# Splitting delta into bfloat16 pieces by the upper halves of its words, with a new plan for the stages between the scans

## The chip, the cores and the metric

The kernel runs on one core of a Trainium2 chip. The metric is device time in microseconds for one execution of the whole program. Before the change the median of 3 runs was 10320.08 us (10318.13 to 10324.31).

## The reference

The input `x` is 8 images of 96 channels and 64 x 64 pixels. Two layers follow. The first is a vision state-space block with four scan directions; the second is linear attention in six heads and a feed-forward net with 8-bit and 16-bit rounding. Cut to what matters here:

```python
# layer 0, per image: L = 4096 pixels, 192 channels, 4 directions k, 16 states n
xz = layernorm(gn(x)) @ in_proj_w.T + in_proj_b      # split into xi and z
xi = silu(depthwise_conv3x3(xi))
xs = four orders of xi                               # rows, columns, and both reversed
dts, Bs, Cs = split(einsum('bkdl,kcd->bkcl', xs, x_proj_w))
delta = softplus(dt_proj(dts) + dt_proj_b)
h[t] = exp(delta[t] * A) * h[t-1] + (delta[t] * u[t]) * B[t]
y[t] = sum over n of C[t] * h[t] + D * u[t]
x = x + (layernorm(sum of the four y) * silu(z)) @ out_proj_w.T + out_proj_b
# layer 1, per image
t = t + linear_attention(layernorm(t))
t = t + ffn(layernorm(t))
```

`delta` is needed twice by the scan: multiplied with the input (`delta * u`), and multiplied with the decay rates `A` under an exponential. The kernel does the second product on TensorE in bfloat16, and keeps its precision by writing each float32 `delta` as a sum of three bfloat16 pieces.

## The kernel before

The images are worked in four pairs. The program is a row of stages: a planned stage for pair 0, the scan of pair 0, a planned stage that finishes pair 0 and prepares pair 1, the scan of pair 1, and so on; a fifth planned stage finishes pair 3. So there are five planned stages and four scans. `scan` (from line 696) is written out by hand, an instruction list of 32 chunks x 4 directions; it reads `delta`'s pieces (`dl`), `delta * u` (`du`) and the states (`bs`, `cs`) from HBM and writes `ys`.

A planned stage is recorded as a list of operations first. `Plan.add` takes for each the engine, a cost in microseconds written in the call, what it reads and writes, which ring of buffers it needs, and a rank (a due time). `Plan.run` then emits the operations: among those that could start within 0.1 us of the earliest on each engine it takes the one of lowest rank, it advances each engine's clock by the written cost, and adds 1.3 us when ScalarE has to change its table of functions. So the costs and ranks decide the order of the instructions on each engine, and nothing else. The chip's engines and the one DMA queue (SP) then take their instructions strictly in that order.

A middle stage holds these parts for the pair that is finished and the pair that is begun:

- `project` (line 419): group norm, layer norm and input projection, 16 chunks of 512 pixels. Ranks rise from 0 to `FRONT`.
- `convolve` (line 513): the depthwise convolution, two thirds on VectorE (lines 537 and 540, 36 instructions of about 1.3 to 2.4 us), one third on TensorE. Ranks from `FRONT` to `CONV`.
- `prepare` (line 587): 32 sets (4 directions x 8 chunks) of 3 tiles of 128 x 512, so 96 tiles. Ranks from `PREP` to 1. A set begins with two matmul groups (lines 637 and 657) that give the states and `delta`'s argument. Each tile then takes: a softplus on ScalarE into `d`; the product `d * u` on VectorE (line 670), which is stored as `du`; and the split of `d` into three pieces in `dp`, stored as `dl`. For the second and fourth direction GpSimd first transposes `u` (line 624).
- `back` (line 935): 16 units, from the sum of the four `ys` (line 982) over the transposition by TensorE (line 996), a layer norm, the gate, the output projection (line 1015) and the attention's sums. Ranks from 0 to `BACK`.
- `tail` (line 1081): 16 units that begin when all of `back` is done; each ends in a store to `out` from GpSimd's last addition (line 1132). Ranks from `TAIL` to `TAIL_END`.

The first stage has no `back` and `tail`, the last has nothing else. The split, as it stands before:

```python
act(..., P[dp][:, :, 0], w(d), AF.Copy, 0.62, ...)                       # ScalarE rounds d
dve(..., tensor_tensor(w(rest), w(d), P[dp][:, :, 0], ALU.subtract))     # line 681, VectorE
act(..., P[dp][:, :, 1], w(rest), AF.Copy, 0.63, ...)                    # ScalarE rounds rest
P.add("POOL", ..., tensor_tensor(P[dp][:, :, 2], w(rest), P[dp][:, :, 1], ALU.subtract))  # line 686
```

Rings limit how many tiles are on their way: three buffers each of `d`, `du` and `dp`, two of `rest`. All stores and loads are issued by SP (line 315), in one queue. The profile names the buffers of the prepare part and of the projection `A`, those of the tail `yd` and `yk`, because they share memory; line 296 is the helper that records every activation.

Of the kernel before, what the change touches and what calls it, by code (L numbers as in the profile page):

```python
# [12 lines left out]
BF16 = mybir.dt.bfloat16  # L13
F8 = mybir.dt.float8e5
AF = mybir.ActivationFunctionType
ALU = mybir.AluOpType
# [3 lines left out]
DIM = 96  # L20
# [17 lines left out]
HQ = TC // 4  # L38
FRONT = 0.13
CONV = 0.27  # L40
PREP = 0.15
BACK = 0.63
TAIL = 0.85
TAIL_END = 1.33
NE = 24
X0 = F - 3 * SEG
WC = 256
# [123 lines left out]
def vss_attn_ffn(ctx: ExitStack, tc: tile.TileContext, a: dict):  # L171
    nc = tc.nc
# [232 lines left out]
    def norm(P, n, src_, read, dst, written, new, hold, rank, **kw):  # L405

        mm(P, 0.9, lambda: nc.tensor.matmul(P["ncp" + n][:DIM], c96, src_(), start=True, stop=True),  # L407
           (read, "w_c96"), ("ncp" + n,), (("ncp" + n, hold),), rank)
        act(P, lambda: P["nsq" + n], lambda: P["ncp" + n][:DIM], AF.Square, 0.6, ("ncp" + n,),
            ("nsq" + n,), (("nsq" + n, "small"),), rank)  # L410
        mm(P, 0.9, lambda: nc.tensor.matmul(  # L411
            P["nvp" + n][:DIM], j96, P["nsq" + n], start=True, stop=True),
           ("nsq" + n, "w_j96"), ("nvp" + n,), (("nvp" + n, "q"),), rank)
# [99 lines left out]
    def convolve(P, xi, ybuf, p1, beside):  # L513
# [10 lines left out]
        for h in range(2):  # L524
# [20 lines left out]
            def taps(h, ns):  # L545
# [11 lines left out]
            P.claims.add(len(P.ops))  # L557
            mm(P, 9.0, lambda h=h, ns=ns, taps=taps: taps(h, ns),
               ("edge1", *[f"pad1#{c}" for c in range(NCH) if h or c <= NCH // 2],
# [27 lines left out]
    def prepare(P, tmp, xi, us, dl, du, bs, cs_, beside):  # L587
# [25 lines left out]
        for o in range(2):  # L613
            for c in range(NCH):
# [14 lines left out]
                for k in (o, o + 2):  # L629
# [3 lines left out]
                    def states(pt, k, u):  # L633
# [8 lines left out]
                    P.unit = f"set.{k}.{c}"  # L642
                    mm(P, 1.9, lambda pt=pt, k=k, u=u, states=states: states(pt, k, u),
                       (*un[0], *un[1], *un[2], "xw"), (pt,), ((pt, "q"),), rank)
# [10 lines left out]
                    def steps_(pqs, k, S):  # L655
# [5 lines left out]

                    mm(P, 1.2, lambda pqs=pqs, k=k, S=S, steps_=steps_: steps_(pqs, k, S),
                       (S, *[f"dtw{at}" for at, *_ in places]), pqs, [(q, "q") for q in pqs], rank)
                    P.unit = None
                    for T in range(3):
                        m = f"{n}.{T}"
                        pq, d, q, dp, rest = "pq" + m, "d" + m, "du" + m, "dp" + m, "rest" + m
                        act(P, lambda d=d: P[d], lambda pq=pq: P[pq], AF.Softplus, 0.675, (pq, "w_dtb"), (d,),
                            ((d, "d"),), rank, "softplus", bias=dtb[:, k, half(T) : half(T) + 1])
                        dve(P, 0.88, lambda q=q, d=d, f=u[T]: nc.vector.tensor_tensor(  # L670
                            P[q], P[d], f(), ALU.mult), (d, *un[T]), (q,), ((q, "du"),), rank)
                        j = slice(c * F // TC, (c + 1) * F // TC)
                        spread(P, 0.26, lambda o, n, k=k, j=j: duv[k, j, o : o + n].rearrange("j p t -> p j t"),
                               T, lambda q=q: P[q].rearrange("p (j t) -> p j t", t=TC), (q,), (), rank)

                        def w(name):
                            return P[name].rearrange("p (j t) -> p j t", t=WC)

                        act(P, lambda dp=dp: P[dp][:, :, 0], lambda d=d, w=w: w(d), AF.Copy, 0.62, (d,),
                            (dp + "#0",), ((dp, "dp"),), rank)  # L680
                        dve(P, 0.88, lambda rest=rest, d=d, dp=dp, w=w: nc.vector.tensor_tensor(  # L681
                            w(rest), w(d), P[dp][:, :, 0], ALU.subtract), (d, dp + "#0"), (rest,),
                            ((rest, "rest"),), rank)
                        act(P, lambda dp=dp: P[dp][:, :, 1], lambda rest=rest, w=w: w(rest), AF.Copy, 0.63,
                            (rest,), (dp + "#1",), (), rank)
                        P.add("POOL", 1.24, lambda rest=rest, dp=dp, w=w: nc.gpsimd.tensor_tensor(  # L686
                            P[dp][:, :, 2], w(rest), P[dp][:, :, 1], ALU.subtract), (rest, dp + "#1"),
                            (dp + "#2",), (), rank)
                        spread(P, 0.39, lambda o, n, k=k, c=c: dlv[
                                   k, c * F // WC : (c + 1) * F // WC, :, o : o + n  # L690
                               ].rearrange("j a p t -> p (j a) t"),
                               T, lambda dp=dp: P[dp].rearrange("p j a t -> p (j a) t"),
                               (dp + "#0", dp + "#1", dp + "#2"), (), rank)
# [241 lines left out]
    def back(P, pair, ys, us, zs, t1, tn, tmp, psm, kept=None):  # L935
# [21 lines left out]
        for i in range(2 * NCH):  # L957
# [55 lines left out]
            def both(dst, src_, w):  # L1013
                for g in range(2):
                    nc.tensor.matmul(P[dst][:DIM], w(g), P[src_][:, g], start=(g == 0), stop=(g == 1))  # L1015

            mm(P, 1.8, lambda mean=mean, yt=yt, both=both: both(mean, yt, lambda g: j192),
               (f"{yt}#0", f"{yt}#1"), (mean,), ((mean, "q"),), rank)
            for g in range(2):
# [3 lines left out]
                    (f"{yt}#{g}",), (f"{g_}#{g}",), ((g_, "g"),), rank)  # L1023
            mm(P, 1.8, lambda yv=yv, g_=g_, both=both: both(yv, g_, lambda g: j192),
               (f"{g_}#0", f"{g_}#1"), (yv,), ((yv, "q"),), rank)
            root(P, n, yv, yrs, "small", rank)
            for g in range(2):
# [5 lines left out]
                    (z3,), (f"{g_}#{g}",), (), rank)  # L1033
            mm(P, 1.8, lambda po=po, g_=g_, both=both: both(po, g_, lambda g: woT[:, g]),
               (f"{g_}#0", f"{g_}#1"), (po,), ((po, "q"),), rank)
# [7 lines left out]
            for h in range(2):  # L1043
# [15 lines left out]

                mm(P, 0.7, lambda pk=pk, to=to, h=h, keys=keys: keys(pk, to, h), (to,), (pk,), ((pk, "q"),), rank)  # L1060
                act(P, lambda kv=kv: P[kv].rearrange("p j s e -> p (j s e)"), lambda pk=pk: P[pk][:, : 4 * DIM],
# [19 lines left out]
    def tail(P, pair, t1, tn, spare, kept):  # L1081
# [10 lines left out]
        for i in range(2 * NCH):  # L1092
# [9 lines left out]
            else:  # L1102
                tf, xa = f"tnsb.{i}", f"tab.{i}"
            P.unit = f"turn.{n}"
            mm(P, 0.9, lambda pa=pa, b=b, tf=tf: nc.tensor.matmul(
                P[pa][:DIM], hm[b], P[tf], start=True, stop=True), (tf, f"hm{b}"), (pa,), ((pa, "q"),), rank)
# [4 lines left out]
            for m in range(3):  # L1111
                p1, h16 = f"pf{m}" + n, f"h16{m}" + n
                mm(P, 0.45, lambda p1=p1, m=m, tq=tq: nc.tensor.matmul(  # L1113
                    P[p1], w1q[:, bass.ts(m, 128)], P[tq], start=True, stop=True), (tq,), (p1,), ((p1, "q"),), rank)
# [7 lines left out]
            def second(p2, hq):  # L1122
                for m in range(3):
                    nc.tensor.matmul(P[p2][:DIM], w2q[:, m], P[hq][:, m], start=(m == 0), stop=(m == 2))

            mm(P, 1.35, lambda p2=p2, hq=hq, second=second: second(p2, hq),
               [f"{hq}#{m}" for m in range(3)], (p2,), ((p2, "q"),), rank)
# [186 lines left out]
```

## Time and profile before

| what | value |
|---|---|
| median of 3 runs | 10320.08 us |
| the profiled execution's own time | 10309.3 us |
| its span, first to last instruction | 10307.5 us |
| planned stages (five) | 0 to 553, 2329 to 3106, 4880 to 5641, 7415 to 8186, 9962 to 10307 us |
| scans (four) | the rest, 1774 to 1776 us each |
| busy share of the span: TensorE, VectorE, ScalarE, GpSimd | 71%, 88%, 68%, 78% |
| L681, VectorE remainder, x384 | 324.2 us, mean 851 ns, median 685 ns |
| L686, GpSimd remainder, x384 | 489.2 us, mean 1280 ns, median 1155 ns |
| L670, product with u, two forms of x192 | means 851 and 1080 ns |
| table loads on ScalarE | 155 x 1283 ns |
| granted TensorE clock, mean | 0.873 |

How to read the views: a group's line gives the source line, the engine, the operation and its tiles, then the busy time and the mean of one instruction. A line of the waits says which engine and line waited for which, the time in total, how often, and the longest. A row by stretch gives, for a piece of the span, the busy time of TensorE (PE), its weight loads (PEld), VectorE (DVE), ScalarE (ACT) and GpSimd (POOL), each with its count of instructions, then the granted TensorE clock, the mean busy share of the DMA engines and the rate they moved. A row of the timeline gives the start, the duration, the engine, the line and operation, and in brackets how long the engine had stood idle and what it had waited for.

### The profile page before, as it was taken

To read this page: it belongs to the slowest core of one execution; us is meant where nothing else is said; L and a number is where in the kernel's file an instruction comes from. 1 tells how busy PE (TensorE), PEld (TensorE's weight loads), DVE (VectorE), ACT (ScalarE), POOL (GpSimd) and SP (SyncE) were. 2 spreads that over 40 slices of the span, in tenths; PEclk is the share of its full clock that TensorE was granted. 3 is DMA by queue.
4 is the path that set the end of the run, shared out by engine and by line. 5 is a ranking of instruction groups with operands and counts; after the bars stand their busy time and mean duration, and the time that the engine had idled before them with its cause. 6 is when DMAs were issued, how large, how long until landed. Compare 5 with 4: busy or idle time off the path is not lost. (4 is left out here: it accounts for less than half of the span.)

```text
span 10307.5 us, 383249 instructions
## 1 busy us (share of the span) xinstructions
PE 7289.4 (71%) x166080; PEld 5185.1 (50%) x166080; DVE 9045.2 (88%) x6688; ACT 7000.9 (68%) x12268; POOL 8011.6 (78%) x2800
## 2 busy tenths in 40 slices
PE   6766666768866666676886666767688567666678
PEld 2155555654315555555432555656543255555554
DVE  6589999997579999999767999999866799999985
ACT  5667777776566777776666777777666677777754
POOL 2499999991259999999125999999713699999971
PEclk7579999898868999989986989898898798999999
DMA  4878887876778888887787788888767788888885
GB/s 127 226 210 214 213 216 212 218 203 146 209 205 210 215 213 217 213 217 189 171 210 203 213 217 212 217 212 217 194 165 206 200 214 214 214 215 216 214 193 104
DMA packets 1593918, 2085.12 MB, mean 202 GB/s; under 512 B 409891, under 2 KB 1050404, under 8 KB 1588644
## 3 DMA queue, kind: packets, MB, share of 16 engines
q1 hardware_dynamic: 1592228, 2060.59, 76.6%
q8 instruction: 1304, 21.36, 1.0%
q14 instruction: 386, 3.16, 0.1%
HBM read 1601.99 MB, written 458.04 MB: 200 GB/s over the span
## 5 line engine op out<-in xcount | busy, mean ns | idle before, releaser
L853 DVE TENSOR_TENSOR_SCAN h<-da,dbu 128x774 f32<-128x774 f32 x4096 | 7026.6, 1759 | 168.1 <-POOL dbu L817 33.1
L817 POOL TENSOR_TENSOR dbu<-dut,bc 128x1536 f32<-128x1536 f32 x2048 | 7081.8, 3572 | 71.8 <-DMA dm<-dl 35.9
L842 ACT ACTIVATE da<-da 128x768 f32<-128x768 f32 x4092 | 3260.7, 797 | 1983.9 <-PE da L835 1969.5
L835 PE MATMUL da<-dm,aw 128*128 128x128 bf16 x24576 | 2281.5, 235 | 2347.3 <-DVE h L853 2081.8
L835 PEld LDWEIGHTS <-aw 128*128 128x128 bf16 x24576 | 1792.2, 104 | 2595.2 <-issue 2308.8
L871 PE MATMUL yp<-h,cw 128*32 128x48 f32 x131072 | 2899.2, 238 | 83.7 <-issue 70.3
L871 PEld LDWEIGHTS yp<-h,cw 128*32 128x32 f32 x131072 | 2409.0, 154 | 528.6 <-issue 207.5
L771 ACT ACTIVATE cw<-bc,blk 128x512 f32<-128x512 f32 x2048 | 1473.1, 721 | 73.0 <-DMA bc<-cs 54.7
L686 POOL TENSOR_TENSOR A<-A 128x512 bf16<-128x512 f32 x384 | 489.2, 1280 | 954.5 <-ACT A L296 912.0
L296 ACT ACTIVATE A<-A 128x512 bf16<-128x512 f32 (+1 forms) x777 | 466.4, 620 | 274.0 <-DVE A L681 228.4
L982 POOL TENSOR_TENSOR yd<-yk 128x768 f32<-128x768 f32 x64 | 120.8, 1888 | 655.3 <-PE q L996 306.4
L879 ACT ACTIVATE yev<-yp 128x384 f32<-128x384 f32 x1024 | 504.7, 493 | 74.6 <-PE yp L871 74.3
L681 DVE TENSOR_TENSOR A<-A 128x512 f32<-128x512 f32 x384 | 324.2, 851 | 174.7 <-ACT A L296 135.7
L814 ACT COPY dbu<-h 128x12 f32<-128x12 f32 x1984 | 409.3, 206 | 0.0
L657 PE MATMUL q<-A 6*64 6x512 f32 x1536 | 331.6, 779 | 74.3 <-ACT A L296 70.4
L624 POOL COPY A<-A 128x512 f32<-128x512 f32 x96 | 142.5, 1504 | 307.8 <-ACT A L296 277.3
L540 DVE SCALAR_TENSOR_TENSOR A<-A,c_convw,A 128x2048 f32<-128x2048 f32 x128 | 299.1, 2355 | 0.6
L996 PEld LDWEIGHTS q<-ident,yd 128*96 128x96 f32 x2048 | 238.6, 165 | 84.1 <-issue 53.1
L670 DVE TENSOR_TENSOR A<-A 128x512 f32<-128x512 f32 x192 | 203.8, 1080 | 77.3 <-ACT A L296 70.8
L996 PE MATMUL q<-ident,yd 128*96 128x128 f32 x2048 | 255.1, 276 | 17.3 <-DVE yd L982 9.5
L637 PE MATMUL q<-A 128*64 128x512 f32 x512 | 209.5, 935 | 77.3 <-ACT A L296 56.6
L296 ACT ACTIVATE small<-hold 96x512 f32<-96x512 f32 x192 | 112.7, 590 | 218.5 <-PE hold L407 218.3
(125 smaller groups left out, 5446.5 us busy)
## 6 DMA issues: line engine op xcount, KB each, us to landing
dut<-du SPq DMA_DIRECT2D x2048, 384.0 KB
dm<-dl SPq DMA_DIRECT2D x1024, 288.0 KB
dl<-A SPq DMA_DIRECT2D x256, 384.0 KB
dm<-dl SPq DMA_DIRECT2D x1024, 96.0 KB
ys<-yev SPq DMA_DIRECT2D x1024, 96.0 KB
du<-A SPq DMA_DIRECT2D x256, 256.0 KB
bc<-cs SPq DMA_DIRECT2D x512, 128.0 KB
bc<-bs SPq DMA_DIRECT2D x512, 128.0 KB
```

What stands on the lines that cost most here:

```text
L296: "ACT", cost, lambda: nc.scalar.activation(dst(), src_(), func, **kw),
L657: nc.tensor.matmul(P[pqs[T]][o : o + 64], dtw[at : at + RK, k, o : o + 64], P[S][at : at + RK], start=True, stop=True,)
L686: P.add("POOL", 1.24, lambda rest=rest, dp=dp, w=w: nc.gpsimd.tensor_tensor(P[dp][:, :, 2], w(rest), P[dp][:, :, 1], ALU.subtract), (rest, ...
L771: nc.scalar.activation(cw[i % 2][:, :, :, m, :].rearrange("p z j t -> p (z j) t"), bc[i][:, 1].rearrange("p z (j t) -> p (z j) t", j=NB), ...
L814: nc.scalar.copy(start, segs(hs[s - 1][:, :, r])[:, :, :, 1 if back else TC])
L817: nc.gpsimd.tensor_tensor(segs(t)[:, :, :, 1:], dut[g].unsqueeze(1) .to_broadcast([128, 2, NI, TC]), bc[s // NB][:, 0, :, bass.ts(c % NB, ...
L835: nc.tensor.matmul(e[:, i], aw[k, r][:, i, z, :], dm[s // 2][:, NI * r + i, bass.ts(c % 2, TC)], start=True, stop=True,)
L842: nc.scalar.activation(e, e, AF.Exp)
L853: nc.vector.tensor_tensor_scan(hs[s][:, w, r][:, d], da[p % 3][:, o : o + W6][:, d], dbu[4 * s + r][:, w][:, d], 0.0, ALU.mult, ALU.add,)
L871: nc.tensor.matmul(y[32 * q : 32 * q + 32, 2 * NE * i : 2 * NE * i + 2 * NE] .rearrange("p (j r i) -> p i j r", j=2, r=NR), w[:, z, :, t], ...
L879: nc.scalar.activation(yev[s][:, :, o : o + 8, :].rearrange("p j i e -> p i j e"), y[:, 0 : 16 * NE].rearrange("p (i j e) -> p i j e", j=2 ...
L996: nc.tensor.matmul(o, P[yd][:, k, j, DIM * g : DIM * g + DIM], ident, start=(k + j == 0), stop=(k + j == 4),)
```

## The change

The change has two parts.

First, the split. A bfloat16 number is the upper half of a float32 word. The new `high(name)` looks at a float32 tile as 2-byte values and takes every second one, so it is the word with its lower half cut off. The first remainder is then `d - high(d)` and the second `rest - high(rest)`; both are VectorE instructions, and neither reads `dp`. ScalarE's two copies of the halves into `dp` stay, and no later remainder reads them. GpSimd's remainder is gone. Pieces are now cut off instead of rounded.

Second, the plan. Six ranks get other values. Costs written for TensorE's groups go up in most places (1.9 to 2.85 and 1.2 to 2.1 in a set, 9.0 to 10.5 for the convolution's taps) and down in two of the tail's. The cost of VectorE's product goes from 0.88 to 0.66, and that of ScalarE's copies from 0.62 and 0.63 to 0.56. These numbers change only the order in which the planned stages' instructions stand.

```diff
-FRONT = 0.13
-CONV = 0.27
-PREP = 0.15
-BACK = 0.63
-TAIL = 0.85
-TAIL_END = 1.33
+FRONT = 0.05
+CONV = 0.35
+PREP = 0.08
+BACK = 0.7
+TAIL = 0.66
+TAIL_END = 1.29
...
-                    mm(P, 1.9, lambda pt=pt, k=k, u=u, states=states: states(pt, k, u),
+                    mm(P, 2.85, lambda pt=pt, k=k, u=u, states=states: states(pt, k, u),
...
-                    mm(P, 1.2, lambda pqs=pqs, k=k, S=S, steps_=steps_: steps_(pqs, k, S),
+                    mm(P, 2.1, lambda pqs=pqs, k=k, S=S, steps_=steps_: steps_(pqs, k, S),
...
-                        dve(P, 0.88, lambda q=q, d=d, f=u[T]: nc.vector.tensor_tensor(
+                        dve(P, 0.66, lambda q=q, d=d, f=u[T]: nc.vector.tensor_tensor(
...
-                        act(P, lambda dp=dp: P[dp][:, :, 0], lambda d=d, w=w: w(d), AF.Copy, 0.62, (d,),
+                        def high(name):
+                            return P[name].bitcast(BF16).rearrange("p (j t o) -> p j t o", t=WC, o=2)[:, :, :, 1]
+
+                        dve(P, 0.66, lambda rest=rest, d=d, w=w, high=high: nc.vector.tensor_tensor(
+                            w(rest), w(d), high(d), ALU.subtract), (d,), (rest,), ((rest, "rest"),), rank)
+                        act(P, lambda dp=dp: P[dp][:, :, 0], lambda d=d, high=high: high(d), AF.Copy, 0.56, (d,),
                             (dp + "#0",), ((dp, "dp"),), rank)
-                        dve(P, 0.88, lambda rest=rest, d=d, dp=dp, w=w: nc.vector.tensor_tensor(
-                            w(rest), w(d), P[dp][:, :, 0], ALU.subtract), (d, dp + "#0"), (rest,),
-                            ((rest, "rest"),), rank)
-                        act(P, lambda dp=dp: P[dp][:, :, 1], lambda rest=rest, w=w: w(rest), AF.Copy, 0.63,
+                        dve(P, 0.66, lambda rest=rest, dp=dp, w=w, high=high: nc.vector.tensor_tensor(
+                            P[dp][:, :, 2], w(rest), high(rest), ALU.subtract), (rest,),
+                            (dp + "#2",), ((dp, "dp"),), rank)
+                        act(P, lambda dp=dp: P[dp][:, :, 1], lambda rest=rest, high=high: high(rest), AF.Copy, 0.56,
                             (rest,), (dp + "#1",), (), rank)
-                        P.add("POOL", 1.24, lambda rest=rest, dp=dp, w=w: nc.gpsimd.tensor_tensor(
-                            P[dp][:, :, 2], w(rest), P[dp][:, :, 1], ALU.subtract), (rest, dp + "#1"),
-                            (dp + "#2",), (), rank)
```

The other lines of the diff change costs alone: the norm's matmuls 0.9 to 1.03, the taps 9.0 to 10.5, the back half's pairs 1.8 to 2.0, its keys 0.7 to 0.86, the tail's first matmul 0.9 to 1.2, its second 0.45 to 0.4 and its third 1.35 to 1.15. The lines below the split stand two lines further down in the new file: the tail's addition on GpSimd is line 1134 there, and the two new remainders are lines 682 and 686.

More of the change, by code (lines that the diff above doesn't have):

```diff
@@ L405, in norm @@
     def norm(P, n, src_, read, dst, written, new, hold, rank, **kw):
-        mm(P, 0.9, lambda: nc.tensor.matmul(P["ncp" + n][:DIM], c96, src_(), start=True, stop=True),
+        mm(P, 1.03, lambda: nc.tensor.matmul(P["ncp" + n][:DIM], c96, src_(), start=True, stop=True),
            (read, "w_c96"), ("ncp" + n,), (("ncp" + n, hold),), rank)
@@ L410, in norm @@
             ("nsq" + n,), (("nsq" + n, "small"),), rank)
-        mm(P, 0.9, lambda: nc.tensor.matmul(
+        mm(P, 1.03, lambda: nc.tensor.matmul(
             P["nvp" + n][:DIM], j96, P["nsq" + n], start=True, stop=True),
@@ L557, in convolve @@
             P.claims.add(len(P.ops))
-            mm(P, 9.0, lambda h=h, ns=ns, taps=taps: taps(h, ns),
+            mm(P, 10.5, lambda h=h, ns=ns, taps=taps: taps(h, ns),
                ("edge1", *[f"pad1#{c}" for c in range(NCH) if h or c <= NCH // 2],
@@ L1015, in both @@
                     nc.tensor.matmul(P[dst][:DIM], w(g), P[src_][:, g], start=(g == 0), stop=(g == 1))
-            mm(P, 1.8, lambda mean=mean, yt=yt, both=both: both(mean, yt, lambda g: j192),
+            mm(P, 2.0, lambda mean=mean, yt=yt, both=both: both(mean, yt, lambda g: j192),
                (f"{yt}#0", f"{yt}#1"), (mean,), ((mean, "q"),), rank)
@@ L1023, in back @@
                     (f"{yt}#{g}",), (f"{g_}#{g}",), ((g_, "g"),), rank)
-            mm(P, 1.8, lambda yv=yv, g_=g_, both=both: both(yv, g_, lambda g: j192),
+            mm(P, 2.0, lambda yv=yv, g_=g_, both=both: both(yv, g_, lambda g: j192),
                (f"{g_}#0", f"{g_}#1"), (yv,), ((yv, "q"),), rank)
@@ L1033, in back @@
                     (z3,), (f"{g_}#{g}",), (), rank)
-            mm(P, 1.8, lambda po=po, g_=g_, both=both: both(po, g_, lambda g: woT[:, g]),
+            mm(P, 2.0, lambda po=po, g_=g_, both=both: both(po, g_, lambda g: woT[:, g]),
                (f"{g_}#0", f"{g_}#1"), (po,), ((po, "q"),), rank)
@@ L1058, in outer @@
                         )
-                mm(P, 0.7, lambda pk=pk, to=to, h=h, keys=keys: keys(pk, to, h), (to,), (pk,), ((pk, "q"),), rank)
+                mm(P, 0.86, lambda pk=pk, to=to, h=h, keys=keys: keys(pk, to, h), (to,), (pk,), ((pk, "q"),), rank)
                 act(P, lambda kv=kv: P[kv].rearrange("p j s e -> p (j s e)"), lambda pk=pk: P[pk][:, : 4 * DIM],
@@ L1104, in tail @@
             P.unit = f"turn.{n}"
-            mm(P, 0.9, lambda pa=pa, b=b, tf=tf: nc.tensor.matmul(
+            mm(P, 1.2, lambda pa=pa, b=b, tf=tf: nc.tensor.matmul(
                 P[pa][:DIM], hm[b], P[tf], start=True, stop=True), (tf, f"hm{b}"), (pa,), ((pa, "q"),), rank)
@@ L1112, in tail @@
                 p1, h16 = f"pf{m}" + n, f"h16{m}" + n
-                mm(P, 0.45, lambda p1=p1, m=m, tq=tq: nc.tensor.matmul(
+                mm(P, 0.4, lambda p1=p1, m=m, tq=tq: nc.tensor.matmul(
                     P[p1], w1q[:, bass.ts(m, 128)], P[tq], start=True, stop=True), (tq,), (p1,), ((p1, "q"),), rank)
@@ L1124, in second @@
                     nc.tensor.matmul(P[p2][:DIM], w2q[:, m], P[hq][:, m], start=(m == 0), stop=(m == 2))
-            mm(P, 1.35, lambda p2=p2, hq=hq, second=second: second(p2, hq),
+            mm(P, 1.15, lambda p2=p2, hq=hq, second=second: second(p2, hq),
                [f"{hq}#{m}" for m in range(3)], (p2,), ((p2, "q"),), rank)
```

## The prediction

> **What bounds the kernel now.** I read the page's busy shares first, then its 40 slices, then the busy time by stretch, then the waits inside the stretches that the change touches, and last the order of the instructions.
>
> ```profile
> DVE  6589999997579999999767999999866799999985
> POOL 2499999991259999999125999999713699999971
> DMA  4878887876778888887787788888767788888885
> ```
>
> The slices show two kinds of stage. Where POOL reads 9 the selective scan runs: VectorE is busy 99 us of each 100 and GpSimd 100. Four such scans take 4 x 1775 us, and the change touches none of their instructions. Between them lie five planned stages, 0 to 553, 2329 to 3106, 4880 to 5641, 7415 to 8186 and 9962 to 10307 us: together 3207 us. There no engine is full, so I ask which wait ends last. The next view has the busy time by stretch (PE, PEld, DVE, ACT, POOL, then clock, DMA share, GB/s): first the prepare part of the first stage, then the second stage in four parts.
>
> ```profile
> 225.00:525.00 300.00, 218.02 (x600) 44.43 (x596) 173.44 (x193) 181.26 (x314) 136.13 (x114) 0.59 0.87 225
> 2329.00:2575.00 246.00, 200.53 (x1423) 105.70 (x1416) 173.63 (x188) 156.77 (x237) 25.74 (x27) 0.90 0.65 151
> 2575.00:2760.00 185.00, 159.71 (x699) 80.30 (x697) 91.34 (x131) 93.42 (x155) 36.78 (x27) 0.88 0.79 209
> 2760.00:3075.00 315.00, 234.94 (x720) 63.55 (x720) 226.77 (x321) 234.88 (x398) 153.99 (x114) 0.71 0.77 208
> 3075.00:3106.00 31.00, 3.06 (x24) 2.52 (x25) 6.13 (x4) 8.41 (x13) 11.76 (x6) 0.50 0.59 150
> ```
>
> I call the four parts of the second stage A (projection and convolution), C (most units of the layer's back half, with the first prepared tiles), D (the rest of the tiles, with the tail units) and E (the scan's start). In D every engine is at 49 to 75% and the DMA below the 225 GB/s of the first stage. What stops them is each other:
>
> ```profile
> POOL A L686 <- ACT A L296: 133.6, 48, 7.2
> ACT A L296 <- DVE A L681: 34.4, 35, 3.3
> DVE A L681 <- ACT A L296: 20.2, 17, 2.6
> ```
>
> ```profile
> SPq L315 <- DVE A L670: 30.5, 25, 3.6
> SPq L315 <- POOL A L686: 29.5, 26, 4.7
> SPq L315 <- ACT A L296: 12.8, 14, 1.7
> ```
>
> The split of delta goes ScalarE, VectorE, ScalarE, GpSimd, store: ScalarE's copy waits for VectorE's remainder and the reverse, and the store queue, served in order, waits for products (L670) and last remainders (L686). SP's waits in D sum to about 103 us. GpSimd also slows VectorE:
>
> ```profile
> 359.55 1.16 POOL L686 TENSOR_TENSOR A<-A 128x512 bf16<-128x512 f32 x1 [2.38 <-ACT A L296]
> 360.08 1.17 DVE L670 TENSOR_TENSOR A<-A,A 128x512 f32<-128x512 f32 x1 [1.33 <-ACT A L296]
> 361.18 0.68 DVE L681 TENSOR_TENSOR A<-A 128x512 f32<-128x512 f32 x1
> ```
>
> A subtraction alone takes 0.68 us, a product begun under L686 1.17. The group means hide this: L681 has median 0.685 and mean 0.851, L670 means 0.851 and 1.080 in its two forms.
>
> **The change, part by part.** A planned stage has 32 sets of 3 tiles, 96 tiles.
>
> *Removed:* 96 x 1.274 us (489.2/384) = 122 us of GpSimd work a stage. It costs GpSimd nothing to lose, but it takes one crossing off the way to each store.
>
> *Added:* 96 remainders on VectorE. Nearest row: L681 without a neighbour, 0.685, so 66 us a stage. Relief in return: L681 96 x 0.166 = 16; L670's first form 48 x 0.167 = 8; of the second form's excess of 0.396 I keep half, since L624's copies remain on GpSimd, 48 x 0.198 = 9.5. Net +33 us a stage.
>
> *Strided halves:* both subtractions and both copies now read 2-byte values 4 bytes apart. No row shows that. The Trainium skill (SBUF — State Buffer, the cachelines note) says that a stride is free while two accesses fall on one 16-byte line; here four do, so I take nothing added: copies 0.62, subtractions 0.685. The upper bound doubles the time per element: VectorE (0.976 for 768 elements, 0.684 for 512) gives 1.14 ns, so +0.58 us an instruction; ScalarE (0.797 for 768, 0.62 for 512) 0.69 ns, so +0.35. Below nothing, a copy of 16-bit data could save some 0.03 us (the f16 evictions took 0.59), 6 us a stage.
>
> *Table loads:* the order shows 54 instead of 47 on ScalarE in each middle stage, 14 and 14 in the first. The row is 1.283 us, and the next activation in D follows at once (a load at 2989.69, work at 2990.99). The skill (ScalarE: Activation LUTs, What ACT_TABLE_LOAD costs) adds a drain of 1.38 us to every switch. By the row, 7 x 1.28 = 9 us; by the rule, 19. I take the row, half of it hidden since ScalarE was busy 75% of D: +5.
>
> *First stage.* The tiles leave at 3.1 us each (300/96). A set stores 1152 KB of pieces, 768 of products and 128 of states: 0.70 MB a tile, 67 MB at 225 GB/s. SP waits for producers only 50 us of 270, in pieces under 1 us mostly. So the DMA bounds this stretch, and the shorter chain only lifts it to what its best 25 us show, 235 GB/s: 300 x (1 - 225/235) = -13. Bounds: 0, and -35 at the 255 GB/s of D's best slices. The prepare part starts no earlier: VectorE still has nearly all 36 convolution steps ahead of its first product.
>
> *Middle stages.* By the order, the old stage has about 21 tiles multiplied when the 16th back unit ends and 75 after it; the new one 36 and 60. It also has one back unit less ahead of the convolution's end. And after the last tile four `out` stores of tail units follow, with the scan's loads behind them on SP; before, only stores of tiles followed the last `out`.
> - A loses one back unit, some 8.4 us of VectorE (0.98 + 2 x 0.74 + 2 x 0.68 + 2 x 0.84 + 2 x 0.75 + 0.74 + 0.69), which was busy there: -9.
> - C gains this unit, 12.8 us of TensorE (205 us for 16 in the last stage), and 15 tiles. TensorE takes 1.94 + 1.67 us a set when warm, so 5 sets 18 us, at C's 86% 21: +34.
> - D loses 15 tiles at 3.1: -46. The rest, 269 us, goes from 208 to the first stage's 225 GB/s as SP's waits shrink: -20. VectorE then has 227 - 27 + 41 - 21 = 220 us in 249, 88%; the convolution stretch shows it at 91%, so it just fits.
> - The end: today the scan's memsets stand between the last tiles:
>
> ```profile
> 3065.14 6.92 POOL L714 MEMSET cw<- 128x8192 f32 x1 [0.48 <-DMA out_dram<-yk]
> 3070.33 6.88 DVE L713 MEMSET cw<- 128x8192 f32 x1 [1.70 <-issue]
> 3072.02 7.86 POOL L686 TENSOR_TENSOR A<-A 128x512 bf16<-128x512 f32 x2
> 3077.14 0.62 DVE L681 TENSOR_TENSOR A<-A 128x512 f32<-128x512 f32 x1
> ```
>
> The last tile's pieces wait for two memsets; in the new order the memsets follow all tiles: -12. But four tail units stay uncovered. The last stage does 16 in 90 us, so 4 x 5.6 = +22.
> Sum: -9 + 34 - 66 - 12 + 22 + 5 = -26, times 3 = -78.
>
> *Last stage:* only its plan changes; TensorE is busy 203 of 218 us in its first part, whatever the order: 0. Scans: 0, though the first loads wait on what ended the stage before.
>
> Total -91 on the profiled execution's own 10309.3 us (span 10307.5): 10218. The median of the runs shown, 10320.08, lies 11 us above that execution, so I forecast 10230.
>
> **Rivals.**
> - *More is freed (0.15).* If D runs at its best slices, 255 GB/s, and C hides the added tiles under TensorE's idle 14%, a middle stage loses 50 and the first 25: 10320 - 175 = 10145, say 10160. For it: SP's 103 us of waits. Against: VectorE at 88%.
> - *The transfers are the limit anyway (0.13).* D stays at 208 GB/s: 3 x 20 and the first stage's 13 vanish, leaving -18 to -30: 10295. For it: DMA shares of 0.77 to 0.87 are near what the stages ever hold.
> - *The uncovered tails eat it (0.12).* A tail unit is a chain of some 30 us; if none of the last four has begun when the last tile leaves, 45 us a stage lie bare instead of 22, and the gain is 22: 10298 to 10325, no change.
> - *The strided halves cost a second turn (0.15), the slower case.* VectorE's pair and ScalarE's pair, in D and the first stage. D's 60 tiles add 60 x 2 x 0.58 = 70 us to VectorE, which then needs 290 us, at 91% 319 instead of 249; C adds about 4. So 74 - 26 = +48 a middle stage, and some +20 in the first: 10320 + 164 = 10485. It decides from about 0.2 us more per instruction, that is when the two remainders average 0.9 us or above. Half of it gives 10390.
> - That the change doesn't do what it says: GpSimd's remainders are gone from its list and VectorE has 96 more a stage, so this is only open for the durations.
>
> **How the numbers follow.** The likeliest case, 10190 to 10280, has 0.45. A measurement of this kernel can tell about 0.2% (21 us) from no change, so the bounds are 10299 and 10341. Faster: 0.45 + 0.15 + most of the 0.13 = 0.72; the rest of that and the tails case give the same, 0.13; slower 0.15. From 10160 to 10325 all but the slower case and a little of the best is held.
>
> **What would show it.** Right: no L686 on GpSimd; subtractions near 0.69 us and products' means well below 0.96; SP's waits in the prepare parts below 60 us; the first stage's prepare part near 287 us at 235 GB/s; middle stages near 745; four tail units after the last tile; scans within 2 us of 1775. Wrong: remainders or copies above 0.9 and 0.7 us; middle stages at 770 or more with SP waiting on VectorE; a bare tail of 40 us; or a last stage that moved by 10 us, which would mean that the plan alone does more than I allow.

## The result, and the profile after

The change is faster: the median went from 10322.19 us (4 runs, 10318.13 to 10332.25) to 10152.76 us (4 runs, 10125.03 to 10156.66), a ratio of 0.9829 (95% interval 0.9810 to 0.9848). That is 169 us. The prediction, 10230 in a range of 10160 to 10325, had the direction and little more than half of the size; the time fell 7 us below the range.

The profiled execution after has a span of 10153.8 us against 10307.5. I cut both spans at the first and last scan instruction of VectorE (L855 after), so that each stage has a length of its own. These cuts lie some microseconds beside the rounded ones used before the change.

| us | first | middle 1 | middle 2 | middle 3 | last | four scans together |
|---|---|---|---|---|---|---|
| before | 549.4 | 774.2 | 758.9 | 769.8 | 345.6 | 7109.6 |
| after | 529.1 | 717.9 | 719.2 | 719.7 | 345.9 | 7122.1 |
| difference | -20.3 | -56.3 | -39.7 | -50.1 | +0.3 | +12.5 |
| forecast | -13 | -26 | -26 | -26 | 0 | 0 |

The differences add up to the 153.7 us of the two spans. (The two profiled executions lie 16 us closer together than the medians do.) So the miss is in the middle stages, 146 us where 78 were forecast.

First the split itself, in the groups of the page (busy time, mean of one, then idle time of the engine before them and what ended most of it). Before:

```profile
L296 ACT ACTIVATE A<-A 128x512 bf16<-128x512 f32 (+1 forms) x777 | 466.4, 620 | 274.0 <-DVE A L681 228.4
L681 DVE TENSOR_TENSOR A<-A 128x512 f32<-128x512 f32 x384 | 324.2, 851 | 174.7 <-ACT A L296 135.7
```

And after:

```profile
L296 ACT ACTIVATE A<-A 128x512 bf16<-128x512 bf16 (+1 forms) x777 | 445.8, 618 | 145.1 <-DMA dl<-A 108.6
L682 DVE TENSOR_TENSOR A<-A 128x512 f32<-128x512 f32 x384 | 287.2, 751 | 88.6 <-ACT A L296 87.2
L686 DVE TENSOR_TENSOR A<-A 128x512 bf16<-128x512 f32 x384 | 279.8, 729 | 83.8 <-DMA dl<-A 81.6
```

All L686 are now VectorE's. The medians of L682 and L686 are 684 and 682 ns, where L681 before had 685; the copies of halves take a mean of 623 ns in their own form, 625 before. Reading every second 2-byte value cost nothing. In the last column of the copies the releaser has changed. Before, they waited most for VectorE's L681 (228.4 us over the program); now they wait most for `dl` stores to free a buffer (108.6 us). The crossing back and forth is gone, and where a copy still waits, the store is mostly what ends last.

Next the first middle stage by stretch, cut at the end of the convolution (A), of the back half's matmuls (C), of the last tile's product (D) and at the scan's start (E). The columns are as ahead of the change. Before:

```profile
2328.40:2570.80 242.40, 198.65 (x1433) 105.38 (x1434) 171.60 (x185) 152.60 (x232) 22.75 (x25) 0.90 0.66 153
2570.80:2791.00 220.20, 189.54 (x800) 90.09 (x799) 113.41 (x159) 123.23 (x202) 51.77 (x39) 0.87 0.78 207
2791.00:3062.70 271.70, 207.54 (x624) 54.65 (x624) 196.85 (x288) 205.80 (x351) 130.17 (x101) 0.72 0.77 206
3062.70:3102.60 39.90, 2.25 (x18) 1.88 (x19) 12.64 (x9) 9.96 (x16) 20.26 (x8) 0.50 0.69 183
```

And after:

```profile
2310.10:2545.70 235.60, 186.98 (x1368) 98.19 (x1368) 165.71 (x175) 148.93 (x223) 20.83 (x24) 0.88 0.63 143
2545.70:2783.10 237.40, 210.49 (x964) 99.94 (x964) 162.18 (x241) 168.75 (x273) 22.36 (x14) 0.91 0.94 247
2783.10:2984.10 201.00, 164.87 (x491) 42.52 (x491) 162.61 (x280) 160.55 (x275) 47.29 (x30) 0.75 0.85 228
2984.10:3028.00 43.90, 16.01 (x52) 6.34 (x52) 25.10 (x44) 20.55 (x38) 15.30 (x9) 0.66 0.66 177
```

The reader is to look at the second row. By the order, 42 tiles instead of 27 have their product by the end of C (the prediction counted 21 and 36; the 15 more are the same). C became only 17 us longer. In it the DMA went from 207 to 247 GB/s and its busy share from 0.78 to 0.94; TensorE's busy time went from 190 to 210 us, at a granted clock of 0.91 instead of 0.87. D lost 71 us.

The same stage as a whole, before and then after, a row from each profile:

```profile
2328.40:3102.60 774.20, 597.98 (x2874) 251.99 (x2875) 494.50 (x638) 491.59 (x799) 224.96 (x171) 0.80 0.73 188
```

```profile
2310.10:3028.00 717.90, 578.35 (x2874) 246.99 (x2875) 515.61 (x735) 498.78 (x806) 105.78 (x76) 0.84 0.80 203
```

Length times DMA share is 774.2 x 0.73 = 565 us before and 717.9 x 0.80 = 574 after (a share has two places, so each is good to 4 us). The bytes are the same, about 146 MB. The DMA's work did not shrink: its idle time did, from 209 to 144 us. No compute engine is full in either row (VectorE works 21 us more after). The question that I took to the runs is what lets the DMA idle in a middle stage. It could be asked of TensorE as well, which after the change is busy for 578 of the 718 us, a share of 0.81 beside the DMA's 0.80.

The waits of the queue SP in part D agree; before, then after:

```profile
SPq L315 <- DVE A L670: 28.4, 20, 3.6
SPq L315 <- POOL A L686: 26.9, 21, 4.7
SPq L315 <- ACT A L296: 11.3, 13, 1.7
```

```profile
SPq L315 <- ACT A L296: 13.2, 26, 2.2
SPq L315 <- DVE A L670: 10.8, 15, 1.6
SPq L315 <- DVE A L686: 10.7, 16, 2.2
```

The products and last remainders, 55 us of SP's waiting before, are 22 us after.

### The profile page after: what moved, and what is told of

It is laid out like the page before. It is cut to its first block, busy times and chain, and to the rows that moved or that the text cites. A ratio compares the mean times of both kernels' runs of the same rounds, so it can differ in the third digit from the quotient of the medians.

```text
span 10153.8 us, 382989 instructions
## 1 busy us (share of the span) xinstructions
PE 7238.0 (71%) x166080; PEld 5184.5 (51%) x166080; DVE 9133.4 (90%) x7072; ACT 7028.9 (69%) x12289; POOL 7542.1 (74%) x2416
## 5 line engine op out<-in xcount | busy, mean ns | idle before, releaser
L855 DVE TENSOR_TENSOR_SCAN h<-da,dbu 128x774 f32<-128x774 f32 x4096 | 7025.9, 1759 | 139.5 <-POOL dbu L819 43.5
L1134 POOL TENSOR_TENSOR yk<-yk,yd 96x512 f32<-96x512 f32 x64 | 100.1, 1565 | 775.7 <-issue 406.0
L296 ACT ACTIVATE A<-A 128x512 bf16<-128x512 bf16 (+1 forms) x777 | 445.8, 618 | 145.1 <-DMA dl<-A 108.6
L682 DVE TENSOR_TENSOR A<-A 128x512 f32<-128x512 f32 x384 | 287.2, 751 | 88.6 <-ACT A L296 87.2
L657 PE MATMUL q<-A 6*64 6x512 f32 x1536 | 301.0, 734 | 78.7 <-ACT A L296 65.5
L686 DVE TENSOR_TENSOR A<-A 128x512 bf16<-128x512 f32 x384 | 279.8, 729 | 83.8 <-DMA dl<-A 81.6
L296 ACT ACTIVATE A<-q,c_dtb 128x512 f32<-128x512 f32 x384 | 253.7, 677 | 7.0 <-PE q L657 6.0
L411 PE MATMUL q<-small,c_j 96*96 96x512 f32 x384 | 230.1, 693 | 28.8 <-ACT small L296 19.1
```

The lines of the kernel that those rows point to most:

```text
L296: "ACT", cost, lambda: nc.scalar.activation(dst(), src_(), func, **kw),
L657: nc.tensor.matmul(P[pqs[T]][o : o + 64], dtw[at : at + RK, k, o : o + 64], P[S][at : at + RK], start=True, stop=True,)
L855: nc.vector.tensor_tensor_scan(hs[s][:, w, r][:, d], da[p % 3][:, o : o + W6][:, d], dbu[4 * s + r][:, w][:, d], 0.0, ALU.mult, ALU.add,)
```

## The experiments

Each kernel was timed in 3 rounds against the kernel before on the same chip; across kernels I compare the ratios, or the spans of the profiled executions. What the expectations call theory 1 and theory 2 is stated in each of them and is not the same throughout.

The table holds all of them beside the two kernels. "Tiles" are those multiplied by the end of the back half, "tails" the tail units that follow the last tile, both by the order of instructions. The stage columns are from the profile: the first stage, the mean of the three middle stages, and their mean DMA idle time (length less length times share) and sum of SP's waits. Ratios are those of the timed runs.

| kernel | split | TensorE costs / ranks | tiles, tails | first | middle | DMA idle | SP waits | ratio (95%) |
|---|---|---|---|---|---|---|---|---|
| before | old | old / old | 27, 0 | 549.4 | 768 | 200 | 325 | 1 |
| the change | new | new / new | 42, 4 | 529.1 | 719 | 149 | 295 | 0.9829 (0.9810 to 0.9848) |
| s1_split_old_plan | new | old / old | 32, 0 | 532.5 | 749 | 182 | 327 | 0.9918 (0.9903 to 0.9933) |
| s2_plan_old_split | old | new / new | 72, 11 | 541.1 | 773 | 203 | 316 | 1.0004 (0.9995 to 1.0013) |
| s3_last_on_gpsimd | new, last remainder on GpSimd | new / new | 51, 0 | 531.2 | 728 | 165 | 276 | 0.9851 (0.9834 to 0.9867) |
| s4_ranks_old | new | new / old | 48, 0 | 530.4 | 759 | 187 | 348 | 0.9939 (0.9924 to 0.9954) |
| s10_gpsimd_old_plan | new, last remainder on GpSimd | old / old | 27, 0 | 532.6 | 774 | 209 | 324 | 1.0008 (0.9999 to 1.0018) |
| s6b_exchange_old_plan | on VectorE, waiting for the copies | old / old | 27, 2 | 544.4 | 766 | 197 | 335 | 0.9982 (0.9972 to 0.9991) |
| s9_old_split_39 | old | new / chosen | 39, 0 | 538.9 | 757 | 187 | 309 | 0.9949 (0.9932 to 0.9966) |
| s5_costs_old | new | old / new | 42, 0 | 532.2 | 756 | 179 | 331 | 0.9948 (0.9931 to 0.9965) |
| s13_nudge | new | new / new, softplus 10 ns dearer | 51, 0 | 530.0 | 742 | 173 | 306 | 0.9899 (0.9885 to 0.9914) |
| s11_tile_costs_old | new | old in the sets only / new | 36, 1 | 530.0 | 726 | 162 | 292 | 0.9856 (0.9841 to 0.9871) |
| s12_tile_costs_new | new | new in the sets only / new | 36, 0 | 538.5 | 767 | 194 | 328 | 0.9988 (0.9979 to 0.9997) |
| s7_front_conv_old | new | new / FRONT and CONV old | 54, 7 | 532.3 | 746 | 182 | 322 | 0.9902 (0.9885 to 0.9918) |

### The two halves of the change alone

`s1_split_old_plan` is the kernel before with the new split and VectorE's and ScalarE's new costs in it; TensorE's costs and the ranks stay:

```diff
 BACK = 0.63
-dve(P, 0.88, ... tensor_tensor(w(rest), w(d), P[dp][:, :, 0], ALU.subtract), (d, dp + "#0"), ...)
+dve(P, 0.66, ... tensor_tensor(w(rest), w(d), high(d), ALU.subtract), (d,), ...)
-P.add("POOL", 1.24, ... tensor_tensor(P[dp][:, :, 2], w(rest), P[dp][:, :, 1], ALU.subtract), ...)
+dve(P, 0.66, ... tensor_tensor(P[dp][:, :, 2], w(rest), high(rest), ALU.subtract), (rest,), ...)
```

> The new split with the ranks and TensorE costs of before; the order has 32 tiles multiplied before the back half ends (before 27, the change 42) and no tail unit after the last tile. Theory 1, the split carries the gain (no GpSimd beside VectorE's subtractions, two crossings fewer to each store): first planned stage near 530 us, middle stages near 730, 10170 to 10210 in all. Theory 2, the plan carries it (tiles put beside TensorE's back half): first stage near 545, middle stages 755 to 770, 10270 to 10320.

It measured 10234.44 us against 10311.67: 77 us.

`s2_plan_old_split` is the opposite, the new TensorE costs and all six ranks with the old split:

```diff
-FRONT, CONV, PREP, BACK, TAIL, TAIL_END = 0.13, 0.27, 0.15, 0.63, 0.85, 1.33
+FRONT, CONV, PREP, BACK, TAIL, TAIL_END = 0.05, 0.35, 0.08, 0.7, 0.66, 1.29
-mm(P, 1.9, ... states(pt, k, u), ...)
+mm(P, 2.85, ... states(pt, k, u), ...)
```

> The old split, with GpSimd's remainder, under the new ranks and costs; the order has 72 tiles multiplied before the back half ends and 11 tail units after the last tile. Theory 1: GpSimd's subtractions still slow VectorE's and the stores wait as before, so the first stage stays at 545 to 552 us, and the middle stages at 760 or above since 11 tail units lie bare: 10300 to 10400. Theory 2: middle stages near 730 to 740, 10200 to 10240.

It measured 10312.01: nothing. So the split alone gives 77 us, the plan alone 0, and both 169. The halves do not add. Each of these three is one order of instructions, and what that is worth is measured further down.

### GpSimd, and the exchange

The split takes two things away: GpSimd's remainder, which slows VectorE beside it, and the waits between ScalarE and VectorE. `s3_last_on_gpsimd` is the change with its last remainder moved back to GpSimd at the old cost; the operands stay the upper halves, so the exchange stays away:

```diff
-dve(P, 0.66, ... nc.vector.tensor_tensor(P[dp][:, :, 2], w(rest), high(rest), ALU.subtract), ...)
+P.add("POOL", 1.24, ... nc.gpsimd.tensor_tensor(P[dp][:, :, 2], w(rest), high(rest), ALU.subtract), ...)
```

> The change with its second remainder back on GpSimd, but by the upper halves, so that it waits for the first remainder alone. If the contention of the two engines and the crossing to GpSimd made the difference: product and first remainder back at means of 0.85 to 1.0 us, the first stage 540 to 548 us, middle stages 740 to 755, 10220 to 10270. If only the exchange between ScalarE and VectorE did, which is gone here too: first stage near 530, middle stages near 720, 10145 to 10175.

It measured 10162.81 against 10311.67; its span of 10166.8 us is 13 above the change's. Yet VectorE pays for its neighbour, as the groups of its page show:

```profile
L686 POOL TENSOR_TENSOR A<-A 128x512 bf16<-128x512 f32 x384 | 465.5, 1216 | 718.0 <-DMA dl<-A 410.4
L682 DVE TENSOR_TENSOR A<-A 128x512 f32<-128x512 f32 x384 | 342.8, 897 | 189.5 <-POOL A L686 116.3
```

L682 takes a mean of 897 ns instead of 751, 56 us over the program. On the other hand VectorE is rid of L686's 280 us, and the order is another one (51 tiles and no tail instead of 42 and 4), so the 13 us are not the price of the neighbour alone. I read from this that the exchange alone had mattered, and two runs under the old plan were to confirm it. `s10_gpsimd_old_plan` is s1 with the same edit, so of the change it has only the end of the exchange. `s6b_exchange_old_plan` has both remainders on VectorE and the exchange (the new lines of its edit, cut):

```diff
+dve(P, 0.66, ... tensor_tensor(w(rest), w(d), P[dp][:, :, 0], ALU.subtract), (d, dp + "#0"), ...)
+dve(P, 0.66, ... tensor_tensor(P[dp][:, :, 2], w(rest), P[dp][:, :, 1], ALU.subtract), (rest, dp + "#1"), ...)
```

> The kernel before with its own plan, and of the change only this: the two copies and the two remainders read the upper halves of words instead of waiting for the copies' results; the last remainder stays on GpSimd at its old cost. The order keeps the old counts: 27 tiles multiplied before the back half's end, no tail after the last tile, but 119 table loads in the planner's list instead of 155. Theory 1 (the exchange between ScalarE and VectorE is what held the store queue): nearly all of the split's 77 us, less about 10 for GpSimd: 10240 to 10260, first stage about 533, middle stages about 750. Theory 2 (GpSimd's remainders and what they cost VectorE held it): as before, 10295 to 10315, first stage 547 to 551, middle stages 760 to 772.

> The opposite half: the old plan, the last remainder on VectorE, so nothing of the split is on GpSimd, but each remainder again waits for the copy of the piece before it (ScalarE, VectorE, ScalarE, VectorE), with the upper halves read by the copies alone. 27 tiles before the back half's end, 2 tails after the last tile, 149 table loads. Theory 1 (the exchange): no gain, 10295 to 10330, first stage 547 or more, middle stages 765 or more, since VectorE now waits twice. Theory 2 (GpSimd): as the split alone, 10230 to 10245, first stage 532, middle stages 747.

They measured 10327.0 and 10303.82 us against 10327.49. The confirmation failed for the whole program, and held for one stage. In the first stage, where only `prepare` follows the projection, s10 has all of the split's gain (532.6; s1 532.5, before 549.4) and s6b little of it (544.4). ScalarE's waits in that stage show why; before (225 to 525 us), then s10, then s6b (both 225 to 500 us):

```profile
ACT A L296 <- DVE A L681: 70.1, 70, 2.2
ACT A L296 <- DMA dl<-A: 20.8, 23, 3.6
```

```profile
ACT A L296 <- DMA dl<-A: 76.2, 52, 3.6
```

```profile
ACT A L296 <- DVE A L684: 62.5, 77, 1.6
ACT A L296 <- DMA dl<-A: 13.7, 17, 4.4
```

Where the exchange is gone, ScalarE's copies wait for the transfers; where it stays, for VectorE. But the exchange is not all of it: the two kernels that keep the old split and have a new plan, s2 and s9, also shorten the first stage, to 541 and 539 us. In the middle stages neither half gains anything: 774 and 766 us against 768, while both together (s1) have 749. In these stages something else decides.

### Is it the order of the tiles, or the written durations?

`s4_ranks_old` keeps the change with the six old ranks:

```diff
-FRONT, CONV, PREP, BACK, TAIL, TAIL_END = 0.05, 0.35, 0.08, 0.7, 0.66, 1.29
+FRONT, CONV, PREP, BACK, TAIL, TAIL_END = 0.13, 0.27, 0.15, 0.63, 0.85, 1.33
```

> The change with the six ranks of before, TensorE costs as in the change; the order has 48 tiles before the back half's end, no tail unit after the last tile, convolution done after 7 back units. Theory 1: within 15 us of the split under the old plan, 10165 to 10210. Theory 2, by the ranks: 10220 or above, middle stages 745 to 760.

10254.07 us: 20 us above s1, which has the old costs too, though the intervals of the two ratios overlap a little. `s5_costs_old` keeps the ranks and takes the old TensorE costs back:

```diff
-mm(P, 2.85, ... states(pt, k, u), ...)
+mm(P, 1.9, ... states(pt, k, u), ...)
-mm(P, 2.1, ... steps_(pqs, k, S), ...)
+mm(P, 1.2, ... steps_(pqs, k, S), ...)
...
```

> The change with the TensorE durations of the old plan; the ranks and the split are the new ones. The order has the change's 42 tiles before the back half's end and no uncovered tail, and 149 table loads instead of 176. If the ranks are the part of the plan that counts: as the change within 15 us, 10140 to 10165, middle stages 715 to 722. If the durations as traced carry it: 10190 or more, middle stages above 730. The fewer table loads could be worth up to 27 x 1.28 = 35 us where ScalarE is on the way, that is 10120 at best.

10262.38 us against 10327.49, a ratio 0.0030 above s1's and 0.0119 (some 123 us) above the change's, with exactly its 42 tiles by the end of the back half and no uncovered tail. Taken as they stand, s4 and s5 say that neither new costs nor new ranks help without the other. And the count of tiles, on which I had built my step for C and D, does not decide. Here are parts C and D of s5's first middle stage, to be held beside the change's second and third row:

```profile
2542.60:2796.00 253.40, 213.64 (x964) 101.64 (x968) 160.21 (x237) 160.39 (x261) 18.51 (x10) 0.89 0.89 230
2796.00:3033.50 237.50, 169.84 (x524) 47.86 (x524) 181.37 (x317) 172.40 (x299) 59.01 (x35) 0.76 0.74 198
```

With the same 964 matmuls in C, C is 33 us longer than in the kernel before, not 17, and D only 34 us shorter, not 71. `s9_old_split_39` asks the same of the old split, with the new costs and PREP, BACK, TAIL and TAIL_END at 0.3, 0.5, 0.6 and 1.25:

> The split of before unchanged, with the new TensorE costs and ranks chosen so that the order is nearly the change's: 39 tiles multiplied before the back half's end and no tail after the last one (the new ranks with the old split gave 72 and 11). If the order alone pays and only the 11 uncovered tails hid it: part C at about 240 GB/s, middle stages 720 to 735, time 10190 to 10230. If the order pays only with the short chain: C at 205 to 225 GB/s with SP's waits in C and D still near 190 us together, middle stages 755 to 772, time 10270 to 10315.

10264.83 us against 10327.49. In the first middle stage part C ran at 243 GB/s, as the first reading had it, but D at 189, and the middle stages took 757 us: between the two readings. The old split too can be planned 63 us faster.

`s11_tile_costs_old` and `s12_tile_costs_new` divide the costs: the two of a set old and the rest new, and the reverse (the two lines of the diff above, one way and the other).

> The change with only the two TensorE durations of a set of tiles as before (1.9 and 1.2 us instead of 2.85 and 2.1); the other TensorE durations, the ranks and the split are the new ones. 36 tiles before the back half's end, one uncovered tail, 182 table loads. If the tiles' durations carry what all the old durations cost (38 us a middle stage): middle stages 745 to 760, total about 10255. If those of the back half carry it: 715 to 725, total about 10155. If it is scatter of the order: in between, with no relation to the part that was changed.

> The complement: the new ranks and split, only the two durations of a set of tiles are the new ones, all other TensorE durations the old. 36 tiles before the back half's end, no uncovered tail, 137 table loads. If the tiles' durations carry the 38 us a middle stage: 715 to 725, total 10140 to 10165. If those of the back half and the convolution carry it: 745 to 760, total about 10255.

10166.25 and 10301.28 us against 10310.44. Taken alone this says that the other durations (back half, convolution, norms, tail) carry the gain and those of the tiles carry none. `s7_front_conv_old` divides the ranks:

```diff
-FRONT = 0.05
-CONV = 0.35
+FRONT = 0.13
+CONV = 0.27
```

> The change with the two ranks of the front and the convolution as before (0.13 and 0.27); PREP, BACK and the tails' ranks new. 54 tiles before the back half's end, 7 uncovered tails, 6 back units instead of 5 ahead of the convolution's end, 188 table loads. If the 26 us that the old ranks cost in the part up to the convolution's end came from these two: that part at 255 to 262 us instead of 236, middle stages 740 or more, total about 10220. If they came from PREP and BACK: that part at 236, middle stages 715 to 730, total 10150 to 10180.

10215.93 us. Its part A takes 261.8 us in the first middle stage, as in s4 (261.5), against 235.6 in the change: under the new costs these two ranks set the end of the convolution. C then ran at 252 GB/s and was 23 us longer, D was 43 us shorter and E 19 longer, and the stage came out 26 longer. As expected of the two ranks in A; not foreseen in the other parts.

### One number moved by 10 ns

All these variants differ in more than their label says, since every edit of the plan sets a different order. `s13_nudge` measures that by itself. It is the change with a duration moved by 10 ns:

```diff
-AF.Softplus, 0.675,
+AF.Softplus, 0.685,
```

> The change with one number of its plan moved by 10 ns, 0.675 to 0.685 us for the softplus; nothing physical differs. The order changes a good deal (51 tiles before the back half's end instead of 42, no uncovered tail instead of 4, 158 table loads instead of 176). Theory 1 (the plan's gain comes from its durations and ranks as such): as the change within 10 us, middle stages 714 to 726, total 10145 to 10165. Theory 2 (a planned stage of this kernel scatters with any change of its order, and the change drew a good one): middle stages anywhere from 715 to 760, at least 15 us a stage from the change, total 10190 or more.

It measured 10211.41 us against 10310.44: a ratio of 0.9899 (0.9885 to 0.9914) where the change has 0.9829, and a span 52 us longer. Its middle stages are 745, 742 and 737 us. Here is its first middle stage, to be held beside the change's row above:

```profile
2307.20:3052.40 745.20, 585.53 (x2874) 253.15 (x2875) 509.84 (x735) 495.11 (x800) 113.73 (x75) 0.83 0.76 196
```

The engines do the same work to within 8 us; the DMA's busy time is 566 us, and its idle 179 instead of 144. The first theory of that expectation, mine up to then, falls: about 23 us a middle stage (742 less 719) went with an edit that has no physical meaning. The second is what the runs show. It is more than one order scatters by itself: the three middle stages of a kernel have the same order, and lie within 2 us of each other in the change, 8 in s13 and 15 in the kernel before.

Seen so, the table reads more simply. The eight plans with the full new split have middle stages of 719, 726, 742, 746, 749, 756, 759 and 767 us, mean 745; the three with the old split 757, 768 and 773, mean 766. In all 42 middle stages the DMA's busy time lies between 561 and 580 us, while the lengths run from 718 to 778. What differs is how long it idles. SP's waits follow that well within the eight plans (295 and 292 us in the two shortest, 306 to 331 in the next four, 348 and 328 in the two longest), and less well across the splits: s2 waits 316 us at 773, s1 327 at 749. The sum does not say which waits found the queue of transfers still full, nor whether the waits make a stage long or come with it.

This is bookkeeping and does not show that the DMA is what limits a middle stage. VectorE's busy time in the eight plans is as constant (505 to 519 us), and TensorE is busy 576 to 603 us there, in most stages longer than the DMA. TensorE's busy time goes with the length: on the whole, the same 2874 matmuls take less of it in the shorter stages, where the granted clock is higher. The six kernels with the shortest middle stages (719 to 749 us) have a mean clock of 0.82 to 0.84 in them, the eight others 0.80 to 0.83. A higher clock may shorten the stage, or a denser stage may get a higher clock; no run separates the two.

## Why the prediction was right or wrong

**First stage, forecast -13, came -20.** The 13 us were right in size and rate: from the start of its first product to that of its last the prepare part takes 282.7 us instead of 295.2, and the DMA runs at 234 GB/s in it, where 235 was forecast. The rest was excluded by "The prepare part starts no earlier", and it does start earlier, before and then after:

```profile
222.33 1.29 DVE L670 TENSOR_TENSOR A<-A,A 128x512 f32<-128x512 f32 x2 [7.82 <-POOL A L624]
215.79 0.68 DVE L670 TENSOR_TENSOR A<-A,A 128x512 f32<-128x512 f32 x1
```

These 6.5 us come with the plan: s2, with the old split, starts at 217.4, and s1, with the old plan, at 226.1. s1 ends nearly as early all the same (532.5), so the two gains do not simply add. s10 and s6b show that under the old plan the exchange makes most of the gain. One sign was missed: SP's waits in the prepare part did not fall, they are 61 us (225 to 500 us) where below 60 was forecast and 54 (225 to 525 us) stood before. Seven of the eight plans with the new split agree at 529 to 533; s12 has 538.5.

**The strided halves, forecast 0.** Right, by the medians above; the slower case is out. **VectorE's extra work**, +33 a stage by my sum, came to 515.6 - 494.5 = +21 in the first middle stage, but not by the terms of that sum: L686 added 70 us where I had 66, L670 and L682 gave back 25 where I had 33. What I had left out are the tail's own VectorE instructions (L1121 and L1132, L1119 and L1130 before), which take 12 us less; the rest lies in small groups and in the overlap of neighbouring instructions.

**A, forecast -9, came -7.** Right. **D, forecast -66, came -71.** Right in sum: 15 tiles gone and 228 GB/s where I had 225. But s5 loses the same 15 tiles in D and gains 34 us at 198 GB/s, so the sum held for this order and not for the count.

**C, forecast +34, came +17. This is the step that failed**, "5 sets 18 us, at C's 86% 21", on top of a back unit at 12.8: the price of the added work in C, 31 us of TensorE, was taken as given by its count. TensorE's busy time rose by 21 us instead. The two groups of the sets, L637 and L657, took 62.9 us in C instead of 52.0, so the 5 sets added 11, not 18; the same matmuls ran shorter, at a granted clock of 0.91 instead of 0.87. L657 in C, before and then after:

```profile
L657 PE MATMUL q<-A 6*64 6x512 f32 x120 | 21.6, 751 | 8.5 <-ACT A L296 8.5
L657 PE MATMUL q<-A 6*64 6x512 f32 x180 | 24.2, 647 | 4.1 <-ACT A L296 3.3 <-DVE ta L1038 0.7
```

And TensorE stood idle for a smaller part, busy 89% instead of 86%, while the DMA, which had idled for 22% of C, took the added stores at 40 GB/s more. Which of these let the other happen is not shown. What the runs do show is that TensorE's work does not fix C's length: s5, with the same tiles in C and 214 us of TensorE where the change has 210, takes 253 us for C, the +33 that I had forecast, and the change 237.

**The end, forecast -12 and +22, came +4.** The -12 was right: the scan's memsets do stand behind all tiles now (the first L714 at 3004.64 us, behind L1132 of the last tail), and E takes 28 us in s1, which has no tail there, where it was 40 before. The four tails were too dear: E takes 44 us with them, so +16. **Table loads:** 176 instead of 155 in the traces. The +5 can't be seen among differences of this size; the kernels with the fewest loads (119 in s10, 128 in s9, 137 in s12) are among the slow ones.

In the first middle stage the terms of C, the end and the table loads were too dear by 17, 6 and up to 5 us, 28 of the 30 us between -26 and -56. But the runs take away more than that: the idea that counts from the order give a stage's length. s5 has the change's count of tiles and stands 37 us above it, s11 has six tiles less and stands 7 above. The change's plan is the best of eight, and the mean of the eight, 745 us, lies 22 below the old kernel's 768, near my -26. I would not call that a hit, since eight plans of one family are few. But it says what the forecast lacked: a width for the draw of the plan, some 16 us of standard deviation a middle stage, the same in all three, so about 48 us of the total. My range ended at 10160 because "more is freed" had its own price there; the scatter of the order was not in it as a case. That rival comes close to the result in number, 50 us a middle stage, but by luck: D ran at 228 GB/s, not at 255, and TensorE's idle time in C fell from 31 to 27 us only.

**Last stage 0, came +0.3; scans 0, came +12.5** in the profiled executions. The 0 of the last stage may be chance: four kernels whose last stage has the same order as before (s1, s5, s10, s12) take 351 to 352 us there, where the one profile of the kernel before has 345.6; the eight with the new costs take 343 to 346. My reason for the 0, that TensorE is busy 203 of 218 us in its first part, was not complete either: the DMA's share is 0.98 there. The scans' instructions are untouched; in the twelve kernels tried the four together lie between 7106 and 7115 us. I have no cause for the difference and used none.

So of the 146 us of the middle stages, an estimate from the means is 3 x (766 - 745) = 63 for the split and the rest for this plan. It is a rough one, from three plans of the old split and eight of the new. What stays open: whether TensorE and its clock or the DMA's queue limits a middle stage; whether back-half durations as traced are really what a good plan needs (the plans with new ranks and these durations have 719, 726, 742 and 746 us, those without 756 and 767, which is more than the one nudge moved, but from six plans); how wide the old split's own scatter is, since it was not nudged; and which of SP's waits empty the queue. A second queue for the `dl` stores, which would test the last directly, was not tried. No run beat the change.

## What to carry to other kernels

Before costing an edit by engine, multiply the stage's length by each engine's share and by the DMA's. Where such a product is the same in all stages of a kind, as the DMA's 561 to 580 us here, a longer stage is one with more idle time and not one with more work, and a price per added piece, read off one part of one order, need not hold in the next (C cost +17 and +33 us for the same tiles). The product does not say which of them is the limit. Where a planner orders the instructions, an edit of one cost is also a new draw; move an unrelated number by 10 ns and time that first, and believe of any single plan only what exceeds that scatter. A half of a change that gains nothing in one plan is no proof that it gives nothing: the new TensorE costs under the old split gained nothing in s2 and 63 us in s9, with other ranks.

## What was not expected of the hardware

TensorE at 89% and a granted clock of 0.91 went together with a DMA at 247 GB/s and 0.94 busy over 237 us (part C of the change), where the highest row by stretch shown of before was 225; in s7 the same part held 252 at 0.96. And VectorE's remainder has a mean of 716 ns (s1) and 751 (the change) without GpSimd's remainders, 842 (s10) and 897 (s3) with them: the price of the neighbour differs with the plan too, perhaps with how often the two meet, which was not counted.
